# A GRU with a routed mixture of experts on one core: a slab's second weights copied by ScalarE, a third buffer for rows to be scattered, and an earlier load of x for the dense blocks

## The chip, the cores and the metric

The kernel runs on one core of a Trainium2 chip. A core has TensorE (PE in the profile; PEld is its weight loading, which runs beside the matmuls), VectorE (DVE), ScalarE (ACT), GpSimd (POOL) and SyncE (SP, which here only issues DMAs). Each has a queue of its own that runs in order. The metric is device time of one execution in microseconds; the kernel before was run seven times, and its median is 1300.95 us (1298.33 to 1306.26).

## The reference, cut to what matters

A GRU runs over x (16 sequences, 256 steps, 512 features) from the state cond. Its 4096 outputs go through a mixture of 8 experts of rank 128, two per token, and the result is added to x. All is fp32.

```python
def cell(h, x):                       # 256 times, one after the other
    i_r, i_z, i_n = jnp.split(x @ W_ih + b_ih, 3, axis=-1)
    h_r, h_z, h_n = jnp.split(h @ W_hh + b_hh, 3, axis=-1)
    r = jax.nn.sigmoid(i_r + h_r)
    z = jax.nn.sigmoid(i_z + h_z)
    n = jnp.tanh(i_n + r * h_n)
    h_new = (1.0 - z) * n + z * h
...
p = softmax(h / norm(h) @ router_w)   # over 8 experts
combine = the two largest p, divided by their sum
out = sum over e of combine[:, e] * (h @ Wa[e] @ Wb[e])
return x + out
```

## The kernel before, in words

**The GRU.** The 256 steps run one after the other in an unrolled loop (32 blocks of 8 steps). In a step (`step`, L937) PE multiplies the transposed state with the r and n weights (`into_rn`, L948), then with the z weights (`into_z`, L958); then it does that part of the next pair's x product that belongs to this step (`gate_in`, L279 and L287); then a little of the mixture's work; then it begins the next step's L948, which needs the new state. The new state comes by a chain through ACT and DVE: tanh for r (ACT L974), two DVE operations for n (L981, L982), tanh for z (ACT L979), tanh for n (ACT L983), then `zh`, `m` and `rows` (DVE L986, L988, L990) and a transpose into `hist` (DVE L993). At the end of every odd step `seed` (L259) lets ACT copy the biases into the PSUM banks of a later pair: two copies.

**The mixture.** Blocks 0 to 28 are sparse: they go in five chunks of 6, 9, 7, 4 and 3 blocks (`CHUNKS`). For each such block `Route` stores the states to DRAM, finds logits and norm (ACT Square at L638, in the fourth step of the block that follows), a softmax (ACT Exp at L308, in the fifth step, as soon as DVE has the largest logit, L305) and the top two. When a chunk is complete, `Chunk` works out a slot for each token and expert, fetches the rows back (`fetch`, L563, from SP's queue into a tile with tag `ht2`) and scatters them to slots in DRAM by indirect DMAs from POOL (`scatter`, L569). `Slab` then takes 128 slots at a time, in two units of 64 that belong to one expert each. There are 78 slabs. A slab loads its rows (L670), copies the two units' first weights out of `wa_sb` (`weights_a`, L694) and second weights out of `wb_sb` (`weights_b`, L703), each unit by a copy of 128x512 whose place depends on the expert's number; that number is read from SBUF into a register by `expert` (L684). Then it transposes (`turn`, L710), multiplies (`down`, L722), evicts (`mid`, ACT L729), multiplies again (`up`, L737), and evicts and stores (`store`, ACT L746 and SP L747). `Combine` loads x (L772), gathers each token's two results (POOL, L776), adds them (DVE L790) and stores (L794).

Blocks 29 to 31 are dense (`Moe`): all experts for all tokens (L858, transposes at L880, evicted by ACT at L887 into tiles `aT`, then L897), x loaded at L823, added at L907, stored at L908.

**What sets the order.** Every such job is an agent with a list of pieces (`plan`). At each step `choose` goes through the agents by rank (routing first, then the chunks' slabs, slabs of a chunk in their order, then the rest) and picks pieces; a piece needs its `gap` in steps and free `room` of what it `takes`, and its PE cost must fit into the step's spare 0.5 us (1.8 us where `gate_in` has nothing to do) or into a credit that makes the work finish in time. PE's part of the picked pieces is issued after the step's own matmuls (`advance(0, ...)`). The other engines' part, `then`, is issued after the step's chain (`advance(1, ...)`), in the order of the agents, and ahead of that odd step's `seed`. So an operation of a piece stands in its engine's queue between this step's chain and the next step's. `keep_order` then holds every engine to the order in which it was written. The planner works with these costs and rooms alone, not with times.

**Buffers in question.** Tag `wbg` has three buffers, `xr` three (used by `Combine` and `Moe`), and `ht2` two (the rows of `fetch`, and the `aT` tiles of `Moe`). `zero`, of 128x512, has a place of its own; it clears the slots in DRAM (`clear`, L213, in steps 6 to 45).

Of the kernel before, what the change touches and what calls it, by code (L numbers as in the profile page):

```python
# [8 lines left out]
FP = mybir.dt.float32  # L9
# [12 lines left out]
P = 128  # L22
# [23 lines left out]
def gru_moe_kernel(  # L46
# [47 lines left out]
    pe, dve, act, pool, sp = nc.tensor, nc.vector, nc.scalar, nc.gpsimd, nc.sync  # L94
    B, T, D = x.shape
    E, _, R = wa.shape
# [5 lines left out]
    HE = E // 2  # L102
# [9 lines left out]
    const = ctx.enter_context(tc.tile_pool(name="const", bufs=1))  # L112
# [12 lines left out]
    moe = ctx.enter_context(tc.tile_pool(name="moe", bufs=2))  # L125
# [29 lines left out]
    for side, src in enumerate((b_ih, b_hh)):  # L155
        for g in (0, 2, 1):
            tag = ("xg", "wbg")[side]
# [19 lines left out]
    wb_sb = const.tile([P, E, D], FP, name="wb_sb")  # L177


    zero = const.tile([P, 512], FP, name="zero")  # L180
    pool.memset(zero, 0.0)
    ones = const.tile([P, 1], FP, name="ones")
    pool.memset(ones, 1.0)
# [173 lines left out]
    class Early:  # L357
# [5 lines left out]
        def load(self):  # L363
            m = self.m
            if self.x is not None:
                return
            self.x = slb.tile([P, D], FP, tag="yg1", bufs=2, name=f"xe_{m}")
            for j in range(NJ):
                for s in range(2):
                    p0 = 32 * j + 16 * s  # L370
                    sp.dma_start(
                        self.x[p0 : p0 + B, 0:P],
                        x[:, 2 * m + s, j * P : (j + 1) * P],
                    )
# [40 lines left out]
        def plan(self):  # L415
            pieces = [
                Piece(then=[("load",)], takes="early"),
                Piece(gap=2, then=[("turn",)], takes="at"),
            ] + [
                Piece(gap=0, cost=c, pe=[("into", what, q)])  # L420
                for what, c in (("rn", 0.43), ("z", 0.22))
                for q in range(NQ)
            ] + [Piece(then=[("store",)], gives="early")]
            pieces[2].gap, pieces[2].takes = 1, ["ps"]
            pieces[9].then, pieces[9].gives = [("keep",)], ["ps", "at"]
            return pieces
# [19 lines left out]
    class Chunk:  # L446
# [112 lines left out]
            self.w = [whi, wlo]  # L559

        def fetch(self, k):
            ht = moe.tile([P, D], FP, tag="ht2", bufs=2, name=f"ht2_{self.c}_{k}")
            sp.dma_start(ht, self.rows[k].rearrange("b t d -> (b t) d"))  # L563
            self.ht = getattr(self, "ht", {})
            self.ht[k] = ht
# [93 lines left out]
    class Slab:  # L659
# [19 lines left out]
            if n == ch.n_slabs - 1:  # L679
                x_users[ch.c % 2] = ch.loads  # L680

        def expert(self, u):
            k = NU * self.n + u
            return pool.value_load(  # L684
                self.chunk.expert[0:1, k : k + 1], min_val=0, max_val=E - 1
            )

        def weights_a(self):
            self.wa = slb.tile(
                [P, NU, NQ, R], FP, tag="wag", bufs=3, name=f"wag_{self.name}"  # L690
            )
            for u in range(NU):
                e = self.expert(u)
                pool.tensor_copy(  # L694
                    self.wa[:, u, :, :],
                    wa_sb[:, :, bass.ds(e, 1), :].rearrange("p q e r -> p (q e) r"),
                )

        def weights_b(self):
            self.wb = slb.tile([P, NU, D], FP, tag="wbg", bufs=3, name=f"wbg_{self.name}")  # L700
            for u in range(NU):
                e = self.expert(u)
                pool.tensor_copy(  # L703
                    self.wb[:, u, :],
                    wb_sb[:, bass.ds(e, 1), :].rearrange("p e f -> p (e f)"),
                )
# [97 lines left out]
    class Moe:  # L804
# [14 lines left out]

        def load(self):  # L820
            i = self.i
            self.xr = moe.tile([P, D], FP, tag="xr", bufs=3, name=f"xr_{i}")
            sp.dma_start(self.xr, x[:, i * TS : (i + 1) * TS, :])  # L823

        def route(self):
# [57 lines left out]
            self.ps["t", s] = ps  # L883

        def evict(self, s):
            self.aT[s] = moe.tile([P, HE, P], FP, tag="ht2", name=f"aT_{self.i}_{s}")
            act.copy(  # L887
                self.aT[s].rearrange("p e t -> p (e t)"),
                self.ps.pop(("t", s)),
            )  # L890
# [19 lines left out]
        def plan(self):  # L910
            pieces = [
                Piece(then=[("prep",)], takes="hc a"),
                Piece(cost=0.6, pe=[("route",)], then=[("soft1",)], gives="a"),
                Piece(cost=0.86, pe=[("down", 0, 0)], then=[("soft2",)], takes="ps"),
                Piece(cost=0.86, pe=[("down", 0, 1)], then=[("soft3",)], takes="a"),
                Piece(gap=0, cost=0.86, pe=[("down", 0, 2)]),
                Piece(gap=0, cost=0.86, pe=[("down", 0, 3)], then=[("scale", 0)],
                      gives="ps"),
            ] + [Piece(gap=0, cost=0.86, pe=[("down", 1, q)]) for q in range(NQ)] + [
                Piece(cost=0.6, pe=[("trans", 0)], then=[("evict", 0)],  # L920
                      takes="ps aT", gives="ps"),
                Piece(cost=0.6, pe=[("trans", 1)], then=[("evict", 1)],
                      takes="ps", gives="ps a hc"),
            ] + [Piece(gap=0, cost=0.86, pe=[("up", e)]) for e in range(E)]
            pieces[6].takes = ["ps"]
            pieces[9].then, pieces[9].gives = [("scale", 1)], ["ps"]
            pieces[12].gap, pieces[12].takes = 1, ["ps"]
            pieces[14].then, pieces[14].takes = [("load",)], ["xr"]
            pieces[19].then, pieces[19].gives = [("store",)], "ps aT xr".split()
            return pieces  # L930


# [207 lines left out]
    for i in range(NB):  # L1140
# [26 lines left out]
        if i < n_sparse:  # L1167
            ch = chunks[-1]
            k = i - (ends[ch.c] // TS - ch.k)
# [55 lines left out]
```

## Time and profile before

The profiled execution took 1297.87 us; its span, from the first to the last instruction, is 1296.1 us. It is one execution, 3.1 us below the median of the seven.

| what | from the profile |
|---|---|
| median of 7 runs | 1300.95 us |
| profiled execution, its span | 1297.87 us, 1296.1 us |
| granted TensorE clock, mean | 0.992 |
| PE busy, PEld busy | 1245.3 us, 895.8 us |
| DVE, ACT, POOL busy | 754.2 us, 386.4 us, 379.0 us |
| of POOL: copies at L694, at L703 | 156 for 100.7 us, 156 for 99.3 us |
| first L948 on a computed state; last | 38.8 us; 1234.7 us |

A group line of the profile reads: line, engine, operation, the tile written, an arrow, the tiles read, the shape, how often; then the busy time in us and the mean of one in ns; then how long the engine had been idle just before them, and what ended that idle time. A timeline line reads: start in us, length in us, engine, line, operation, tiles, shape, how many were merged; in brackets the idle time before it and its releaser. A line of the waits reads: who waited, for whom, us in total, times, the longest. A busy PE is not PE at its limit: its matmuls overlap and their ends are modelled.

### The profile page before, as it was taken

The page shows a single profiled execution, that of the slowest core. Times are in us where ns is not written, and L with a number is a line of the kernel's source. Part 1 is how long each engine was busy: PE and PEld are TensorE (multiplying, and loading weights), DVE is VectorE, ACT ScalarE, POOL GpSimd, SP SyncE. Part 2 cuts the span into 40 slices and gives each one's busy share as a digit, 9 for nine tenths or more (in the row PEclk, how much of TensorE's full clock was granted, in tenths as well). Part 3 has the DMA queues.
Part 4 walks back from the last instruction along what each step waited for, and adds up shares of the span by engine and source line. Part 5 has one row for each costly group of instructions (what it writes and reads, how often), then busy time and mean ns, then how long its engine had stood idle before and what let it go on. Part 6 is the DMA issues. An engine that isn't in the chain of part 4 may idle for free.

```text
span 1296.1 us, 73564 instructions
## 1 busy us (share of the span) xinstructions
PE 1245.3 (96%) x32494; PEld 895.8 (69%) x32494; DVE 754.2 (58%) x2691; ACT 386.4 (30%) x1338; POOL 379.0 (29%) x668
## 2 busy tenths in 40 slices
PE   6899999999999999999999999999998988989998
PEld 3577777776777777777777777777786767766753
DVE  0455555565655555556556665566566766676643
ACT  1222222322333333233333333333333323333220
POOL 2000000023311111112424332225245554465453
PEclk7999999999999999999999999999999999999999
DMA  8532422124221112212535433225355765565454
GB/s 201 147 119 87 132 74 89 52 83 136 74 61 49 48 52 61 57 48 76 192 101 152 142 105 85 60 93 182 96 146 159 207 214 150 171 183 164 142 177 129
DMA packets 142300, 152.17 MB, mean 117 GB/s; under 512 B 21846, under 2 KB 98710, under 8 KB 141980
## 3 DMA queue, kind: packets, MB, share of 16 engines
q1 hardware_dynamic: 132560, 117.01, 31.2%
q0 software_dynamic: 9280, 30.42, 7.3%
q8 instruction: 254, 4.16, 1.4%
q14 instruction: 66, 0.54, 0.1%
q10 hardware_dynamic: 140, 0.05, 0.0%
HBM read 82.11 MB, written 65.27 MB: 114 GB/s over the span
## 4 chain that ended last, share of the span: by engine, by line
PE 87%; DVE 7%; DMA 3%; issue 1%; ACT 1%; SPq 0%; POOL 0%; POOLq 0%; ACTq 0%; DVEq 0%
PE rn L948 35%; PE z L958 17%; PE rn L279 14%; PE z L287 7%; PE at_ps L722 4%; PE y_ps L737 4%; DVE rows L990 1%; PE a_ps L858 1%; PE gi L387 1%; DVE zh L986 1%; PE o_ps L897 1%; DVE m L988 1%; DMA whh<-in_L_cond_W_hh_dram 1%; PE rt L351 1%; DVE hist L993 1%
## 5 line engine op out<-in xcount | busy, mean ns | idle before, releaser
L948 PE MATMUL rn<-whh,hist 128*32 128x256 f32 x8160 | 497.3, 383 | 29.2 <-DVE hist L993 27.8
L948 PEld LDWEIGHTS rn<-whh,hist 128*32 128x32 f32 x8160 | 251.8, 110 | 207.0 <-DVE hist L993 57.6
L279 PE MATMUL rn<-wih,xT 128*32 128x256 f32 x3712 | 291.8, 382 | 9.7 <-DMA wih<-in_L_cond_W_ih_dram 7.9
L981 DVE SCALAR_TENSOR_TENSOR n<-r,rn 128x128 f32<-128x128 f32 x256 | 73.5, 287 | 352.4 <-ACT r L974 351.4
L958 PE MATMUL z<-whh,hist 128*32 128x128 f32 x8160 | 274.1, 273 | 0.0
L958 PEld LDWEIGHTS z<-whh,hist 128*32 128x32 f32 x8160 | 238.2, 110 | 42.5 <-issue 1.4
L974 ACT ACTIVATE r<-rn 128x128 f32<-128x128 f32 x256 | 71.1, 278 | 428.4 <-PE rn L948 426.2
L287 PE MATMUL z<-wih,xT 128*32 128x128 f32 x3712 | 193.5, 274 | 0.0
L287 PEld LDWEIGHTS z<-wih,xT 128*32 128x32 f32 x3712 | 126.7, 111 | 77.5 <-issue 2.2
L703 POOL COPY wbg<-wb_sb 128x512 f32 x156 | 99.3, 647 | 107.8 <-PE y_ps L737 90.4
L279 PEld LDWEIGHTS rn<-wih,xT 128*32 128x32 f32 x3712 | 115.9, 111 | 11.6 <-DMA wih<-in_L_cond_W_ih_dram 5.0
L986 DVE SCALAR_TENSOR_TENSOR zh<-z,h 128x128 f32<-128x128 f32 x255 | 83.9, 329 | 66.9 <-ACT z L979 65.2
L694 POOL COPY wag<-wa_sb 128x512 f32 x156 | 100.7, 655 | 63.8 <-PE at_ps L722 45.9
L979 ACT ACTIVATE z<-z 128x128 f32<-128x128 f32 x256 | 71.1, 278 | 153.8 <-PE z L958 153.8
L640 POOL TENSOR_TENSOR nrm<-ss,half 128x1 f32<-128x1 f32 x29 | 16.3, 563 | 342.9 <-ACT ht L638 321.8
L722 PE MATMUL at_ps<-xgT,wag 128*32 128x64 f32 x4992 | 90.2, 219 | 4.0 <-issue 1.6
L722 PEld LDWEIGHTS at_ps<-xgT,wag 128*32 128x32 f32 x4992 | 84.1, 110 | 8.5 <-issue 3.4
L990 DVE SCALAR_TENSOR_TENSOR rows<-zh,m 128x128 f32<-128x128 f32 x256 | 82.9, 324 | 8.9
L737 PE MATMUL y_ps<-wbg,at 128*32 128x256 f32 x1248 | 87.2, 380 | 0.1
L993 DVE STREAM_TRANSPOSE hist<-rows 128x128 f32<-128x128 f32 x256 | 79.8, 312 | 8.7
L1001 DVE STREAM_TRANSPOSE h<-hist 128x128 f32<-128x128 f32 x256 | 79.7, 311 | 8.7
L988 DVE SCALAR_TENSOR_TENSOR m<-z,n 128x128 f32<-128x128 f32 x256 | 82.3, 322 | 1.0 <-ACT n L983 0.7
(136 smaller groups left out, 1042.1 us busy)
## 6 DMA issues: line engine op xcount, KB each, us to landing
xg<-x_slots SPq DMA_DIRECT2D x312, 64.0 KB
y_slots<-y SPq DMA_DIRECT2D x78, 256.0 KB
ht<-H SPq DMA_DIRECT2D x58, 256.0 KB
x_slots<-zero SPq DMA_DIRECT2D x40, 256.0 KB
x<-in_x_dram SPq DMA_DIRECT2D x256, 32.0 KB
xr<-in_x_dram SPq DMA_DIRECT2D x32, 256.0 KB
out_dram<-xr SPq DMA_DIRECT2D x32, 256.0 KB
H<-rows SPq DMA_DIRECT2D x232, 32.0 KB
```

What stands on the lines that cost most here:

```text
L279: pe.matmul(rn[32 * j : 32 * j + 32, 0 : 3 * P].rearrange("p (g d) -> p g d", g=3)[:, 0:3:2, :], lhsT=xts[m][:, q, :], rhs=w[:, 0:3:2, j, ...
L287: ins = pe.matmul(zb[32 * j : 32 * j + 32, 0:P], lhsT=xts[m][:, q, :], rhs=w[:, 1, j, :], start=False, stop=(q == NQ - 1), skip_group_chec ...
L694: pool.tensor_copy(self.wa[:, u, :, :], wa_sb[:, :, bass.ds(e, 1), :].rearrange("p q e r -> p (q e) r"),)
L703: pool.tensor_copy(self.wb[:, u, :], wb_sb[:, bass.ds(e, 1), :].rearrange("p e f -> p (e f)"),)
L722: pe.matmul(self.ps[c32, us], lhsT=self.wa[:, u, q, c32], rhs=self.xt[:, q, us], start=(q == 0), stop=(q == NQ - 1),)
L737: pe.matmul(self.ps[c32, half], lhsT=self.at[:, c32], rhs=self.wb[:, 32 * c // U, half], start=True, stop=True,)
L948: pe.matmul(rn[32 * j : 32 * j + 32, 0 : 2 * P].rearrange("p (g d) -> p g d", g=2), lhsT=hT[:, q, :], rhs=w(q, j)[:, 0:3:2, :], start=Fals ...
L958: pe.matmul(zb[32 * j : 32 * j + 32, 0:P], lhsT=hT[:, q, :], rhs=w(q, j)[:, 1, :], start=False, stop=(q == NQ - 1), skip_group_check=True,)
L986: dve.scalar_tensor_tensor(zh, z, 1.0, hrow, ALU.add, ALU.mult)
L988: dve.scalar_tensor_tensor(m, z, 1.0, n, ALU.subtract, ALU.mult)
L990: dve.scalar_tensor_tensor(hn, zh, 0.5, m, ALU.mult, ALU.subtract)
L993: dve.transpose(hist[:, t, :, lo : lo + 32], hn.rearrange("p (q c) -> p q c", q=NQ))
```

## The change

A slab's `weights_b` is issued on ACT in place of POOL: the two reads of an expert's number and the two copies. `weights_a` stays on POOL. Tag `ht2` gets three buffers; `zero` becomes the first tile in that ring, and the dense blocks' x goes through it too, so that `xr` is left to `Combine` alone. The dense blocks' load of x moves from the third `up` piece (14) to the second transpose piece (11), which is one planner step sooner, behind the second `evict`, and takes no room any more. `CHUNKS`, `ROOM` and all else stay.

```diff
-    zero = const.tile([P, 512], FP, name="zero")
+    zero = moe.tile([P, 512], FP, tag="ht2", bufs=3, name="zero")
...
         def fetch(self, k):
-            ht = moe.tile([P, D], FP, tag="ht2", bufs=2, name=f"ht2_{self.c}_{k}")
+            ht = moe.tile([P, D], FP, tag="ht2", bufs=3, name=f"ht2_{self.c}_{k}")
...
-        def expert(self, u):
+        def expert(self, eng, u):
             k = NU * self.n + u
-            return pool.value_load(
+            return eng.value_load(
...
-                e = self.expert(u)
+                e = self.expert(pool, u)
                 pool.tensor_copy(
                     self.wa[:, u, :, :],
...
-                e = self.expert(u)
-                pool.tensor_copy(
+                e = self.expert(act, u)
+                act.copy(
                     self.wb[:, u, :],
...
         def load(self):
-            self.xr = moe.tile([P, D], FP, tag="xr", bufs=3, name=f"xr_{i}")
+            self.xr = moe.tile([P, D], FP, tag="ht2", bufs=3, name=f"xr_{i}")
...
-            self.aT[s] = moe.tile([P, HE, P], FP, tag="ht2", name=f"aT_{self.i}_{s}")
+            self.aT[s] = moe.tile([P, HE, P], FP, tag="ht2", bufs=3, name=f"aT_{self.i}_{s}")
...
-            pieces[14].then, pieces[14].takes = [("load",)], ["xr"]
-            pieces[19].then, pieces[19].gives = [("store",)], "ps aT xr".split()
+            pieces[11].then.append(("load",))
+            pieces[19].then, pieces[19].gives = [("store",)], "ps aT".split()
```

## The prediction

> **What bounds the kernel now.** The page's chain ends on PE for 87% of the span, so the first question is whether PE is full or waits. The second view is the timeline, here the change from one step to the next:
>
> ```profile
> 1062.22 1.93 PE L948 MATMUL rn<-whh,hist 128*32 128x256 f32 x32 [1.93 <-DVE hist L993]
> ...
> 1063.43 0.30 ACT L308 ACTIVATE ex<-ls,mx 128x8 f32<-128x8 f32 x1 [3.65 <-DVE mx L305]
> 1063.64 0.19 ACT L308 ACTIVATION_READ_ACCUMULATOR ex<-ls,mx 128x1 f32 x1
> 1064.22 0.28 ACT L974 ACTIVATE r<-rn 128x128 f32<-128x128 f32 x1 [0.40 <-PE rn L948]
> ...
> 1066.63 1.93 PE L948 MATMUL rn<-whh,hist 128*32 128x256 f32 x32
> 1066.85 0.27 ACT L729 COPY at<-at_ps 128x128 f32<-128x128 f32 x1 [1.27 <-PE at_ps L722]
> 1067.01 0.49 ACT L259 COPY rn<-gl 128x384 f32<-128x384 f32 x1
> 1067.53 0.27 ACT L259 COPY z<-gl 128x128 f32<-128x128 f32 x1
> 1068.63 0.28 ACT L974 ACTIVATE r<-rn 128x128 f32<-128x128 f32 x1 [0.83 <-PE rn L948]
> ```
>
> ACT's r begins 2.00 us after PE's L948 (1064.22 against 1062.22), and the next L948 begins 4.41 after the last (1066.63). From r to r this 4.40 us comes back in most of the first hundred steps, with and without work for the mixture: it is the chain's own length. So in such a step a late r delays the next step by as much; PE's filler only covers a delay where a step is longer because PE was last. 256 x 4.40 is 1126 us; the loop ran from 38.8 to about 1239, so some 70 us are steps that are longer. One cause is seen in a third view, the groups by line:
>
> ```profile
> L703 POOL COPY wbg<-wb_sb 128x512 f32 x156 | 99.3, 647 | 107.8 <-PE y_ps L737 90.4
> L986 DVE SCALAR_TENSOR_TENSOR zh<-z,h 128x128 f32<-128x128 f32 x255 | 83.9, 329 | 66.9 <-ACT z L979 65.2
> L990 DVE SCALAR_TENSOR_TENSOR rows<-zh,m 128x128 f32<-128x128 f32 x256 | 82.9, 324 | 8.9
> ...
> L988 DVE SCALAR_TENSOR_TENSOR m<-z,n 128x128 f32<-128x128 f32 x256 | 82.3, 322 | 1.0 <-ACT n L983 0.7
> ```
>
> Undisturbed, the three take 291, 291 and 283 ns in the timeline. Where POOL copies beside them they take longer:
>
> ```profile
> 1075.33 0.66 DVE L986 SCALAR_TENSOR_TENSOR zh<-z,h 128x128 f32<-128x128 f32 x1 [0.26 <-ACT z L979]
> 1075.92 0.69 DVE L988 SCALAR_TENSOR_TENSOR m<-z,n 128x128 f32<-128x128 f32 x1
> 1076.64 1.13 DVE L990 SCALAR_TENSOR_TENSOR rows<-zh,m 128x128 f32<-128x128 f32 x1
> ```
>
> In that stretch POOL had L703 copies from 1074.69 to 1075.85 and L694 copies from 1075.80 on.
>
> **Gain: POOL's copies leave DVE's chain.** The means give (329-291)x255 + (322-283)x256 + (324-291)x256 = 9.7 + 10.0 + 8.4 = 28 us lost on these three, all on the chain. Laid over POOL's rows, 9.1 us of it stand beside L703 copies alone, 4.2 beside L703 and another POOL operation; the rest is L694's and others'. I take 13 us: L703's part, with the shared part whole, since what is left on POOL then runs with less backlog. Bounds: 0 (L694 copies move into the freed time and meet the same DVE operations) and 28 (all collisions come of backlog).
>
> **Cost: ACT's copies stand between the tanh of n and the next r.** All 78 slabs' pairs move. In POOL's queue a read of an expert's number is four sequencer operations, of 288, 152, 18 and 46 ns at the median, and paces the copies:
>
> ```profile
> 1232.54 1.31 POOL L694 COPY wag<-wa_sb 128x512 f32 x2
> ```
>
> The second copy starts 1.31 - 0.61 = 0.70 us after the first. ACT's own 128x512 copies run 0.53 from start to start where nothing is between:
>
> ```profile
> 1242.35 0.59 ACT L746 COPY y<-y_ps 128x512 f32<-128x512 f32 x1 [0.32 <-PE y_ps L737]
> 1242.88 0.59 ACT L887 COPY aT<-aT_ps 128x512 f32<-128x512 f32 x1
> ```
>
> So I count, from the start of the ACT instruction ahead: 0.70 to the first copy, 0.70 to the second, 0.53 until the next instruction, 1.93 in all, and 1.40 for each further slab. ACT never read a register or a register's address here, so this is a price from POOL's rows. Bounds: the reads run ahead and cost nothing (1.06 for two copies), or each read waits until the copy ahead is over (0.7 + 0.6 from copy to copy; the longest read in the trace took 1143 ns).
>
> Which steps? The planner's rules, followed step by step, put 74 pairs into 67 steps of the loop and 4 behind it; ACT's rows give what stands ahead of them.
>
> (a) Ten steps, 12 slabs: the fifth step of a block, with Exp ahead. Exp waits for DVE's L305, which comes after the state, so it ends late: in the first fence at 1063.64, then 1063.64 + 1.93 = 1065.57 against an r at 1064.22: 1.35 late. Eight such are 10.8, two with two slabs 2 x 2.75 = 5.5: 16 us.
>
> (b) Sixteen odd steps with an `at` eviction ahead, which waits for PE's filler, and the two seeds behind: in the fence 1066.85 + 1.93 = 1068.78, the seeds 0.52 + 0.27 more, r at 1069.57 in place of 1068.63: 0.94 late. Where PE has the `at` piece first, the eviction is earlier and little is lost. Row by row the sixteen are 11.1 us late, of which steps with PE last hide 0.8: 10.3 us. The seeds are 1.8 us late too; PE's `gate_in` behind them then starts some 0.5 us late, inside the delay of r.
>
> (c) Three odd steps with two slabs, or with Square ahead and no `at`: 2.4 + 2.4 + 1.8 = 6.6 us.
>
> (d) Twenty-five even steps with `at` ahead and no seeds: 0.22 + 1.93 = 2.15 against 2.00, in the steps where `at` waited; 1.2 us in all.
>
> (e) Thirteen steps with neither: the copies follow the tanh of n at 3.05 after L948, end at 4.98 (5.8 with seeds), and r is due at 6.40: 0. The cover is 0.6 us.
>
> The sum is 16 + 10.3 + 6.6 + 1.2 = 34 us. With reads for nothing the same rows give 16.5, with reads that wait 77.
>
> Two sentences of the Trainium skill bear on this. The trace has ACT busy for 30% of the span, so by its share 156 copies would fit in for nothing; "Perfetto Trace Analysis", section "Optimizing Scalar/DVE Operations", says that an unsaturated ScalarE may still cause bubbles on other engines, and advises to break its instructions up; by the share the sum would be 13 us faster, by the rows above it is slower. The trace's register read of 288 ns can be set beside "Runtime: NRT & Kernel Launch", section "Instruction fetch mechanics", which gives about 200 ns for a register read from HBM; by it, as an estimate, copies would be 0.09 us closer and the cost some 5 us less; the row is what I use.
>
> **The third buffer.** SP waits in order for scatters to let go of `ht2`, and POOL for the rows:
>
> ```profile
> SPq L563 <- DMA x_slots<-ht,ilo: 67.3, 13, 12.1
> ```
>
> With two buffers a fetch waits for the scatter issued in the same step, with three for that of the step before, so most of the 67 us goes. Behind it stand x loads, stores and slab loads; PE's waits on these are about 1 us each, and POOL's 39.7 us of waits for `ht` end no PE wait either. I take 0 (up to 3 us of fewer late POOL copies). `zero`'s clears end before step 46, the first fetch comes later: 0.
>
> **The dense loads.** Three DMAs of the same size go one planner step sooner on SP. The ring holds two `aT` and one x per block, so a load waits for the block before to be stored: that store is issued at 1259.26 and 1276.26, the loads' uses are at 1275.54 and 1291.61. What is behind such a load on SP (other stores and loads of `Combine`) waits a few us at most. Tail after the loop: ACT has about 10.6 us of work in 61; four slabs' copies shift evictions by some tenths. I take 0.5 us.
>
> **The sum.** 34 - 13 + 0 + 0.5 = 21.5 us on 1297.87: 1319.4. The median lies 3.1 above the profiled execution: 1322.5.
>
> **Rivals.**
> - Forecast, ACT's price and POOL's relief as taken: 1322.5, from about 1305 (26 - 22) to 1343 (46 - 4). Chance 0.77.
> - The reads on ACT wait for the copies ahead: 77 - 13 = 64, so 1365. For it: on POOL some reads took up to 1143 ns beside a copy. Against: the median is 288 beside running copies. Chance 0.07.
> - A wash: reads run ahead (16.5) and relief is 13 to 18: 1300 to 1304. That the third buffer frees nothing belongs here too, as I count it for nothing. Chance 0.10.
> - Faster: backlog is the cause of nearly all collisions. 28 of relief against 16.5 is -11.5: 1289. Its place is DVE L986 to L990 in the last 300 us, where POOL is busiest (147 us of 285 from 950 to 1235). It decides once the relief exceeds ACT's cost by 4 us. Against: half of POOL's copies stay, and (a) is late by the order of the queue whatever a read costs. Chance 0.06.
>
> About 0.3% (4 us) is what a measurement can tell from no change. Faster 0.06, the same 0.09, slower 0.85. The range 1302 to 1345 holds the forecast's own bounds and the upper half of the wash; it leaves out 0.07 + 0.06 + 0.05.
>
> **What would show it.** In the profile after: ACT copies of `wbg`, 0.70 apart in pairs; r's idle time no longer ended by PE in the steps of (a) and (b), with L948 to L948 some 1 to 1.4 us longer there and PE waiting for `hist`; means of L986, L988 and L990 near 310 ns; SP's wait at L563 under 15 us. It is wrong if the reads overlap the instruction ahead, if L694's copies collide as often as both did, or if the time in the tail changes by more than 2 us.

## The result, and the profile after

The kernel after takes 1311.61 us (median of 19 runs, 1307.16 to 1315.25), the kernel before 1301.34 us (46 runs on the same chips): ratio 1.0074 [1.0063, 1.0085]. It is slower, as forecast, but by 10.3 us and not by 21.5. Its profiled execution took 1310.17 us with a span of 1308.4 us, 12.3 us more than that of before; the granted clock is 0.992 in both. From line 181 on every line of the kernel after carries a number one higher.

First the chain that ended last, by engine:

```profile
PE 78%; DVE 8%; ACT 5%; DMA 3%; issue 3%; SPq 2%; ACTq 1%; POOL 0%; POOLq 0%; DVEq 0%
```

Before, PE held 87% of it and ACT 1%. Part of what PE held has gone to ACT and its queue, and the line list of the page puts 2% of the span on the new copies. The group of r before, and then the groups by line of after:

```profile
L974 ACT ACTIVATE r<-rn 128x128 f32<-128x128 f32 x256 | 71.1, 278 | 428.4 <-PE rn L948 426.2
```

```profile
L704 ACT COPY wbg<-wb_sb 128x512 f32 x156 | 96.4, 619 | 34.7 <-issue 30.6
...
L991 DVE SCALAR_TENSOR_TENSOR rows<-zh,m 128x128 f32<-128x128 f32 x256 | 78.5, 307 | 8.9
...
L987 DVE SCALAR_TENSOR_TENSOR zh<-z,h 128x128 f32<-128x128 f32 x255 | 77.4, 304 | 63.2 <-ACT z L980 62.7 <-issue 0.3
L989 DVE SCALAR_TENSOR_TENSOR m<-z,n 128x128 f32<-128x128 f32 x256 | 76.3, 298 | 5.8 <-ACT n L984 5.4
...
L975 ACT ACTIVATE r<-rn 128x128 f32<-128x128 f32 x256 | 70.8, 277 | 346.0 <-PE rn L949 345.6
```

Two things moved against each other. The DVE means fell from 329, 322 and 324 ns to 304, 298 and 307: (25 x 255 + 24 x 256 + 17 x 256) ns is 16.9 us, the gain. And ACT waited for PE before r for 346 us in place of 426: ACT arrives later at r, because copies stand ahead of it. The timeline shows both kinds of step in which this happens:

```profile
1067.60 1.93 PE L949 MATMUL rn<-whh,hist 128*32 128x256 f32 x32
...
1068.81 0.30 ACT L309 ACTIVATE ex<-ls,mx 128x8 f32<-128x8 f32 x1 [2.26 <-DVE mx L306]
1069.01 0.19 ACT L309 ACTIVATION_READ_ACCUMULATOR ex<-ls,mx 128x1 f32 x1
...
1069.46 1.28 ACT L704 COPY wbg<-wb_sb 128x512 f32 x2 [0.26 <-issue]
...
1070.65 0.27 ACT L975 ACTIVATE r<-rn 128x128 f32<-128x128 f32 x1
...
1072.22 0.27 ACT L730 COPY at<-at_ps 128x128 f32<-128x128 f32 x1 [0.31 <-PE at_ps L723]
...
1072.88 1.28 ACT L704 COPY wbg<-wb_sb 128x512 f32 x2 [0.40 <-issue]
...
1072.96 1.93 PE L949 MATMUL rn<-whh,hist 128*32 128x256 f32 x32 [0.81 <-DVE hist L994]
...
1074.07 0.48 ACT L260 COPY rn<-gl 128x384 f32<-128x384 f32 x1
...
1074.58 0.27 ACT L260 COPY z<-gl 128x128 f32<-128x128 f32 x1
...
1074.96 0.28 ACT L975 ACTIVATE r<-rn 128x128 f32<-128x128 f32 x1
```

The first step is of class (a): Exp waits for DVE, the copies wait for Exp, and r comes 3.05 us after L949 (1070.65 against 1067.60) where 2.00 is free of delay. PE pays at once: it stands 0.81 us for `hist` before the next L949. In the second the copies stand behind an `at` eviction, and seeds stand behind the copies. SP's wait at the fetch fell from 67.3 us to 15.4, as the third buffer promised:

```profile
SPq L564 <- DMA x_slots<-ht,ilo: 15.4, 7, 4.4
```

To say where the 12.3 us lie I cut each of 254 steps of the loop into three: from L949's weight load on the new state to r, from r to the end of `hist`, from there to the next L949. Undisturbed they are 2.00, 2.35 and 0.05 us, 4.40 together. The table sums what goes beyond that, from the rows of one profiled execution each (us).

| kernel | r late | chain longer | PE last | loop | behind the loop |
|---|---|---|---|---|---|
| before | 16.9 | 33.0 | 26.8 | 1194.3 | 63.0 |
| after | 42.3 | 15.8 | 30.8 | 1206.6 | 63.2 |
| change (rounded after the sum) | +25.5 | -17.2 | +4.1 | +12.3 | +0.3 |

The middle column holds more than DVE's three operations, for instance ACT's wait before the tanh of z. From the start of the tanh of n to the end of `hist`, where the three stand, the 254 steps take 357.1 us before and 340.4 after: 16.7 of the 17.2 us lie there.

### The profile page after: what moved, and what is told of

It reads as the page before. It is cut to its first block, busy times and chain, and to the rows that moved or that the text cites. A ratio compares the mean times of both kernels' runs of the same rounds, so it can differ in the third digit from the quotient of the medians.

```text
span 1308.4 us, 73461 instructions
## 1 busy us (share of the span) xinstructions
PE 1247.4 (95%) x32494; PEld 891.1 (68%) x32494; DVE 732.1 (56%) x2691; ACT 479.2 (37%) x1494; POOL 279.2 (21%) x512
## 4 chain that ended last, share of the span: by engine, by line
PE 78%; DVE 8%; ACT 5%; DMA 3%; issue 3%; SPq 2%; ACTq 1%; POOL 0%; POOLq 0%; DVEq 0%
PE rn L949 31%; PE z L959 15%; PE rn L280 12%; PE z L288 6%; PE at_ps L723 4%; PE y_ps L738 4%; ACT wbg L704 2%; PE o_ps L898 2%; PE a_ps L859 2%; DVE rows L991 1%; PE gi L388 1%; DVE m L989 1%; DVE hist L994 1%; PE rt L352 1%; DMA whh<-in_L_cond_W_hh_dram 1%
## 5 line engine op out<-in xcount | busy, mean ns | idle before, releaser
L949 PE MATMUL rn<-whh,hist 128*32 128x256 f32 x8160 | 496.3, 383 | 31.0 <-DVE hist L994 27.6
L949 PEld LDWEIGHTS rn<-whh,hist 128*32 128x32 f32 x8160 | 249.8, 110 | 211.7 <-DVE hist L994 61.0
L959 PE MATMUL z<-whh,hist 128*32 128x128 f32 x8160 | 274.0, 273 | 3.6 <-issue 3.5
L959 PEld LDWEIGHTS z<-whh,hist 128*32 128x32 f32 x8160 | 237.3, 110 | 46.9 <-issue 5.2
L987 DVE SCALAR_TENSOR_TENSOR zh<-z,h 128x128 f32<-128x128 f32 x255 | 77.4, 304 | 63.2 <-ACT z L980 62.7
L704 ACT COPY wbg<-wb_sb 128x512 f32 x156 | 96.4, 619 | 34.7 <-issue 30.6
L991 DVE SCALAR_TENSOR_TENSOR rows<-zh,m 128x128 f32<-128x128 f32 x256 | 78.5, 307 | 8.9
L984 ACT ACTIVATE n<-n 128x128 f32<-128x128 f32 x256 | 77.7, 303 | 15.8 <-DVE n L983 15.6
```

The source lines that it names most:

```text
L704: act.copy(self.wb[:, u, :], wb_sb[:, bass.ds(e, 1), :].rearrange("p e f -> p (e f)"),)
L949: pe.matmul(rn[32 * j : 32 * j + 32, 0 : 2 * P].rearrange("p (g d) -> p g d", g=2), lhsT=hT[:, q, :], rhs=w(q, j)[:, 0:3:2, :], start=Fals ...
L959: pe.matmul(zb[32 * j : 32 * j + 32, 0:P], lhsT=hT[:, q, :], rhs=w(q, j)[:, 1, :], start=False, stop=(q == NQ - 1), skip_group_check=True,)
L984: act.activation(n, n, AF.Tanh)
L991: dve.scalar_tensor_tensor(hn, zh, 0.5, m, ALU.mult, ALU.subtract)
```

## The experiments

On the chips of all experiments but first_in_loop the kernel before takes 1372 to 1376 us in place of 1301, with the same code; its granted clock there is 0.981 to 0.994 over all runs (on the chip of first_in_loop 0.991 to 0.995). So only ratios to the kernel before on the same chip are compared, and the table of steps has a part of its own for such a chip further down. A ratio of 0.01 is 13.7 us there.

| kernel | ratio to before | | kernel | ratio to before |
|---|---|---|---|---|
| act_only | 1.0060 [1.0039, 1.0082] | | act_first | 1.0054 [1.0033, 1.0076] |
| act_only_b | 1.0052 [1.0034, 1.0070] | | act_first_b | 1.0057 [1.0038, 1.0076] |
| rest_only | 1.0078 [1.0053, 1.0102] | | first_no_ring | 0.9965 [0.9949, 0.9980] |
| rest_only_b | 1.0117 [1.0100, 1.0134] | | first_no_ring_b | 0.9973 [0.9950, 0.9996] |
| after_b | 1.0146 [1.0125, 1.0166] | | first_in_loop | 0.9964 [0.9950, 0.9979] |
| before_b | 1.0003 [0.9983, 1.0023] | | ring_only | 1.0107 [1.0072, 1.0142] |
| no_copy | 0.9881 [0.9853, 0.9910] | | ring_only_b | 1.0109 [1.0074, 1.0144] |
| no_reads | 0.9923 [0.9902, 0.9944] | | dense_only | 1.0015 [0.9992, 1.0037] |
| pool_twice | 1.0186 [1.0157, 1.0215] | | ring_spaced | 1.0028 [0.9999, 1.0058] |

### The halves of the change

My theory was that ACT's copies make the whole difference and that the third buffer and the dense loads make none. The rival was that these cost something too. act_only has the copies alone:

```diff
-    e = self.expert(u)
-    pool.tensor_copy(self.wb[:, u, :], ...)
+    e = self.expert(act, u)
+    act.copy(self.wb[:, u, :], ...)
```

> Against before: ScalarE takes over the second weights, nothing else changes. Theory (the whole result is ScalarE's later r against fewer GpSimd collisions on VectorE's chain; the ring and the earlier loads give nothing): +9 to +13 us, as in the whole change, ratio 1.007 to 1.010. Rival (the third buffer gives part of the relief, since some steps without any copy became shorter and one Square came earlier): without it +14 to +18 us, ratio 1.011 to 1.014.

rest_only has all the rest, with the copies on POOL:

```diff
-    zero = const.tile([P, 512], FP, name="zero")
+    zero = moe.tile([P, 512], FP, tag="ht2", bufs=3, name="zero")
...
-            ht = moe.tile([P, D], FP, tag="ht2", bufs=2, name=f"ht2_{self.c}_{k}")
+            ht = moe.tile([P, D], FP, tag="ht2", bufs=3, name=f"ht2_{self.c}_{k}")
...
-            self.xr = moe.tile([P, D], FP, tag="xr", bufs=3, name=f"xr_{i}")
+            self.xr = moe.tile([P, D], FP, tag="ht2", bufs=3, name=f"xr_{i}")
...
-            pieces[14].then, pieces[14].takes = [("load",)], ["xr"]
+            pieces[11].then.append(("load",))
```

> Against before: the ring of three, zero in it, and the dense blocks' x sooner, with GpSimd copying as before. Theory: 0 to -1 us, ratio 0.999 to 1.000; SyncE's wait for scatters still falls from 67 to about 15 us. Rival (the third buffer gives part of the relief): -3 to -6 us, ratio 0.995 to 0.998, with fewer microseconds lost on VectorE's chain.

Both were run again, and with them the kernel after and the kernel before as kernels of their own (no edit to either).

> ScalarE's copies without the ring and the earlier loads, once more. Where the kernel before takes about 1301 us: +9 to +13 us if the ring gives nothing, +14 to +18 us if it gives part of the relief.

> The ring and the earlier loads without ScalarE's copies, once more: in the first run of it the kernel before took 1372 us on that chip, 5% above its 1301 elsewhere, and engines stood still for want of instructions around the scatters. On a chip where the kernel before takes about 1301 us: 0 to -4 us (ratio 0.997 to 1.000) if the ring gives nothing or a little; +8 to +12 us (1.006 to 1.009) if the ring itself costs what it cost in the first run.

> The whole change beside its parts on one chip. On a chip like that of the first comparison: ratio 1.0074 again. On one like that of the first four experiments: about the sum of the parts measured there, 1.006 and 1.008, so 1.012 to 1.016, if the parts add up.

> The kernel before itself, for its profile on these chips: ratio 1.00. If engines that stand still for want of instructions around the scatters make up the 70 us between 1373 and 1301, the profile has such idle time without a releaser, but less of it than the kernels with the ring of three.

The copies cost 1.0052 to 1.0060, the rest 1.0078 and 1.0117, both 1.0146. act_only lies below both ranges that were expected of it and rest_only above both of its own. On these chips the parts add up, as was expected of after_b, and the larger one is the part that I had put at nothing. That also means that 1.0146 here and 1.0074 in the result are not the same sum; the last group of experiments is about this.

### How large the relief is

no_copy leaves out the choice of the expert for the second weights: `up` multiplies by a fixed expert's block of `wb_sb` in place, and nobody copies.

```diff
-    rhs=self.wb[:, 32 * c // U, half],
+    rhs=wb_sb[:, (NU * self.n + 32 * c // U) % E, half],
```

> The kernel before without any copy of the second weights on any engine: the second product reads a fixed expert's weights in place (the choice of the expert is left out). This is the relief alone, with no cost on ScalarE. Theory (the traces: 17 us less on VectorE's chain and 6 us from earlier r): -17 to -23 us, ratio 0.983 to 0.987. Rival (the relief is what was forecast): -10 to -14 us, 0.989 to 0.992.

pool_twice is the whole change with each `wag` copy made twice:

```diff
+    for _ in range(2):
         pool.tensor_copy(self.wa[:, u, :, :], ...)
```

> The whole change, but each copy of the first weights on GpSimd is made twice (same data, same place), so GpSimd has again as many copies as before the change, while ScalarE's part is untouched. Theory (GpSimd's copies beside VectorE's chain were what the change relieved): the relief of 17 to 22 us goes and the time is +25 to +35 us against before, ratio 1.019 to 1.027. Rival (the relief has another cause, as the third buffer): the time stays within 4 us of the whole change, ratio 1.005 to 1.011.

no_copy gives 0.9881, 16 us of 1373, between its two expected ranges: POOL's second copies, with their reads and whatever waits for them, cost the kernel before that much. Its groups by line (the file is shorter, so these are zh, rows and m again under other numbers):

```profile
L980 DVE SCALAR_TENSOR_TENSOR zh<-z,h 128x128 f32<-128x128 f32 x255 | 78.6, 308 | 106.0 <-ACT z L973 97.1 <-issue 8.9
...
L984 DVE SCALAR_TENSOR_TENSOR rows<-zh,m 128x128 f32<-128x128 f32 x256 | 77.2, 302 | 8.9
L982 DVE SCALAR_TENSOR_TENSOR m<-z,n 128x128 f32<-128x128 f32 x256 | 74.1, 290 | 1.4 <-ACT n L977 0.9 <-issue 0.2
```

They stand at 329, 310 and 307 ns in before_b. In pool_twice the collisions come back in part, by the same view:

```profile
L992 DVE SCALAR_TENSOR_TENSOR rows<-zh,m 128x128 f32<-128x128 f32 x256 | 82.6, 323 | 8.9
L988 DVE SCALAR_TENSOR_TENSOR zh<-z,h 128x128 f32<-128x128 f32 x255 | 78.3, 307 | 83.9 <-ACT z L981 73.5 <-issue 9.8
L990 DVE SCALAR_TENSOR_TENSOR m<-z,n 128x128 f32<-128x128 f32 x256 | 77.8, 304 | 6.3 <-ACT n L985 5.4 <-issue 0.2
```

Against after_b (301, 305, 295) these are (22 x 256 + 2 x 255 + 9 x 256) ns, 8.4 us, for 156 added copies, and from the tanh of n to the end of `hist` the steps take 346.7 us against 338.5. So the added copies bring back part of what the moved ones took away. The ratio, 1.0186, is 0.4% above after_b's and just under the expected 1.019. It doesn't price the collisions by themselves: in these two executions PE was last for 11 us more in pool_twice, while the time from r to the tanh of z was 22 us shorter in all.

### What the reads of an expert's number cost

no_reads is act_only with a fixed expert for each unit, so it leaves out the choice of the expert as well; ACT makes the same 156 copies, but reads no register.

```diff
-    e = self.expert(act, u)
-    act.copy(self.wb[:, u, :], wb_sb[:, bass.ds(e, 1), :]...)
+    e = (NU * self.n + u) % E
+    act.copy(self.wb[:, u, :], wb_sb[:, e, :])
```

> ScalarE copies the second weights as in the change, without the ring, but of a fixed expert, so no expert's number is read on ScalarE (the choice of the expert is left out). Theory (the copies' place costs, and the reads between them about half): ScalarE's lateness falls from about 31 to about 15 us, so -3 to -9 us against before, and 12 to 16 us below the run with reads. Rival (the reads run beside the copies and cost next to nothing): +4 to +10 us, as with reads.

0.9923 against no_copy's 0.9881: copies alone cost 6 us. act_only lies 1.3% above no_reads, so the reads cost about 18 us; ACT's whole price on these chips is 24 us. The reads are the larger part of the price, though no engine counts them as busy; the expectation had them at about half. The two kernels ran on different chips of the slower kind, each beside the kernel before.

### The place in ACT's queue

The prediction put the cost on the order of the queue: copies stand behind evictions that wait for PE or DVE, though they themselves need nothing of the step. If so, the same copies ahead of these evictions should be nearly free, since ACT is idle there. act_first is the whole change with this order:

```diff
 def advance(phase, picked):
+    if phase:
+        for a, p in picked:
+            if ("weights_b",) in p.then:
+                a.weights_b()
     for a, p in picked:
         for what, *args in (p.then if phase else p.pe):
-            getattr(a, what)(*args)
+            if what != "weights_b":
+                getattr(a, what)(*args)
```

> The whole change, but a step's copies of the second weights stand first among ScalarE's work of that step, ahead of Exp, Square and the evictions, so right behind the tanh of n. Theory (a copy costs by its place in the queue): they start about 3.1 us after the step's first matmul, end at about 5.0, and the next r is due at 6.4; only the four steps with two slabs are late, by under 1 us each. The 17 us of relief on VectorE's chain stay: -10 to -17 us against before, ratio 0.987 to 0.992. Rival (ScalarE's copies cost by their number or disturb the chain wherever they stand): +5 to +12 us, ratio 1.004 to 1.009.

> ScalarE's copies first in their step, once more, for the same reason. Where the kernel before takes about 1301 us: -10 to -17 us (0.987 to 0.992) if a copy costs by its place in the queue; +5 to +12 us (1.004 to 1.009) if it costs wherever it stands.

first_no_ring has the same order with the buffers and dense loads of before:

> ScalarE's copies first in their step, with two buffers, zero and the dense loads as before. Theory (the copies cost by their place; the ring of three costs by itself on the chips of these runs, where the kernel before takes about 1373 us): -5 to -12 us there, ratio 0.991 to 0.996; where it takes 1301 us, -10 to -17 us, 0.987 to 0.992. Rival (a copy on ScalarE costs wherever it stands): +5 to +10 us.

> The same kernel as first_no_ring (ACT's copies at the head of the step's work, buffers as before), again. If its 0.9965 is more than a chance of one chip: 0.993 to 0.999. If the place in the queue is worth nothing: 1.005 as act_only.

The order takes the whole change from 1.0146 to 1.0054 and 1.0057, and the copies alone from 1.0052 and 1.0060 to 0.9965 and 0.9973: the sign turns. By itself act_first lies in the range of its rival, since its expectation had put the third buffer at nothing; it is first_no_ring, without that buffer, that decides. It gained a little less than was expected of it. Behind the loop, though, first_no_ring took 69.2 us where before_b took 64.0. In first_in_loop the order holds within the 256 steps only:

```diff
-    if phase:
+    if phase and now <= T:
...
-            if what != "weights_b":
+            if what != "weights_b" or now > T:
```

> ACT's copies at the head of a step's work within the 256 steps, in the old order behind them; buffers as before. first_no_ring's loop was 9.6 us shorter than that of the kernel before on the same chip and its tail 5.2 us longer (69.2 against 64.0). If the order in the tail is what made the tail longer: ratio 0.991 to 0.995, tail near 65 us. If the tail is longer because of what the loop leaves over for it: 0.996 to 0.998 as first_no_ring.

It fell on a chip where the kernel before takes 1300.54 us; it takes 1295.83, 0.9964. The stretch behind the loop is back at 63.5 us, so the order there seems to have made it longer; but the sum is not better than first_no_ring's, because the loop gained 6.3 us here against 9.6 there, by one execution of each. That part of the expectation missed. Its timeline and the group of r:

```profile
1071.44 0.30 ACT L983 ACTIVATE n<-n 128x128 f32<-128x128 f32 x1
...
1072.01 1.28 ACT L703 COPY wbg<-wb_sb 128x512 f32 x2 [0.27 <-issue]
...
1072.80 1.93 PE L948 MATMUL rn<-whh,hist 128*32 128x256 f32 x32
...
1073.20 0.58 ACT L746 COPY y<-y_ps 128x512 f32<-128x512 f32 x1
1073.68 0.27 ACT L729 COPY at<-at_ps 128x128 f32<-128x128 f32 x1
...
1073.84 0.49 ACT L259 COPY rn<-bias 128x384 f32<-128x384 f32 x1
...
1074.36 0.27 ACT L259 COPY z<-bias 128x128 f32<-128x128 f32 x1
...
1074.80 0.28 ACT L974 ACTIVATE r<-rn 128x128 f32<-128x128 f32 x1 [0.17 <-PE rn L948]
```

```profile
L974 ACT ACTIVATE r<-rn 128x128 f32<-128x128 f32 x256 | 70.9, 277 | 382.0 <-PE rn L948 380.7 <-issue 1.2
```

The copies start 0.57 us after the tanh of n, while DVE still makes the state. Even with two evictions and two seeds behind them, ACT still waits 0.17 us for PE before r, 2.00 us after L948. By the steps: r late 19.1 us (42.3 in after), chain 16.2 (15.8 in after), PE last 35.2. The relief is kept, ACT's price is gone, and PE takes back 8.4 us of it against before.

### The third buffer and the dense loads

These two were 0 in my sum. ring_only is rest_only without its last two edits (x stays in `xr` and is loaded in piece 14). dense_only keeps the earlier load, gives x one buffer of its own and `ht2` two:

```diff
-            self.xr = moe.tile([P, D], FP, tag="ht2", bufs=3, name=f"xr_{i}")
+            self.xr = moe.tile([P, D], FP, tag="xd", bufs=1, name=f"xr_{i}")
...
-            ht = moe.tile([P, D], FP, tag="ht2", bufs=3, name=f"ht2_{self.c}_{k}")
+            ht = moe.tile([P, D], FP, tag="ht2", bufs=2, name=f"ht2_{self.c}_{k}")
```

> Three buffers of tag ht2 with zero as the first tile of the ring, POOL copying as before, the dense blocks' x in tag xr and loaded in piece 14 as before. If the third buffer is what cost rest_only its 0.8 to 1.2% (scatters closer together, and engines standing still beside them): ratio 1.007 to 1.012 to the kernel before, POOL L570 scatters back to back, waits of over 5 us on an engine that name no instruction. If the earlier dense load is what cost: 0.998 to 1.002.

> Two buffers of tag ht2 as before, with zero as the ring's first tile; the dense blocks' x in one buffer of its own, loaded in piece 11 without taking room; POOL copying as before. If the third buffer is the cost: 0.998 to 1.002. If the earlier dense load is the cost (it stands on SP's queue until the block before is stored, with stores and loads of Combine behind it): 1.007 to 1.012, with the excess in the last 100 us.

ring_spaced is rest_only with a chunk's scatters two planner steps apart. Its slabs stay where they were, so some of them load rows that are scattered only later; the operations are the same.

```diff
     pieces[2 + m].then.append(("scatter", m))
+    if m:
+        pieces[2 + m].gap = 2
```

> rest_only with the scatters of a chunk two planner steps apart in place of one, so that the third buffer can't bring them together. If the density of scatters is the cost: 0.999 to 1.004, and waits that name no instruction as in the kernel before or shorter. If it is the earlier dense load, or a cost of the third buffer that doesn't depend on the spacing: 1.007 to 1.012 as in rest_only.

> The same kernel as ring_only. Its cost of 1.07% was measured on a chip where the kernel before takes 1372 us and where engines stand still for want of instructions beside scatters. If the cost belongs to that standing still, and the run falls on a chip where the kernel before takes about 1300 us: 0.997 to 1.003, with no step of over 9 us at the scatters. If the third buffer costs by itself: 1.007 to 1.012 on such a chip too. On a chip of 1372 us it only repeats: 1.007 to 1.014.

It is the buffer: 1.0107 and 1.0109 alone, the earlier load 1.0015 with an interval that holds 1, and with the scatters spaced 1.0028 (the weaker proof, since some slabs there no longer wait for scatters). The timeline of ring_only has the place:

```profile
284.00 1.20 POOL L570 DMA_INDIRECT x_slots<-ht,ihi  x1 [8.03 <-DVE ilo L526]
...
285.32 0.28 ACT L975 ACTIVATE r<-rn 128x128 f32<-128x128 f32 x1 [2.77 <-PE rn L949]
...
285.51 0.99 POOL L570 DMA_INDIRECT x_slots<-ht,ilo  x1 [0.31 <-issue]
...
286.81 0.98 POOL L570 DMA_INDIRECT x_slots<-ht,ihi  x1 [0.31 <-issue]
286.82 0.45 PE L288 MATMUL z<-wih,xT 128*32 128x128 f32 x4 [0.31 <-issue]
...
289.37 0.97 POOL L570 DMA_INDIRECT x_slots<-ht,ihi  x1 [0.30 <-issue]
...
291.93 0.98 POOL L570 DMA_INDIRECT x_slots<-ht,ihi  x1 [0.30 <-issue]
...
292.86 0.28 ACT L980 ACTIVATE z<-z 128x128 f32<-128x128 f32 x1 [7.26 <-remote]
```

Eight scatters run without a pause, and ACT waits 7.26 us before the tanh of z for something that the profile can't name ("remote"; PE's z matmuls, L959, had ended at 285.73), while PE takes its matmuls in groups of one to five with gaps of "issue". That step takes 12.8 us; in dense_only, where the fifth scatter waits 2.57 us for its rows, 7.6, in ring_spaced 8.7. Now the same step and the same scatters in the kernel after, in the execution of the result:

```profile
283.33 1.20 POOL L570 DMA_INDIRECT x_slots<-ht,ihi  x1 [8.03 <-DVE ilo L526]
...
284.26 0.28 ACT L975 ACTIVATE r<-rn 128x128 f32<-128x128 f32 x1 [2.37 <-PE rn L949]
...
284.84 0.99 POOL L570 DMA_INDIRECT x_slots<-ht,ilo  x1 [0.31 <-issue]
...
285.13 0.28 ACT L980 ACTIVATE z<-z 128x128 f32<-128x128 f32 x1 [0.60 <-PE z L959]
...
286.14 0.98 POOL L570 DMA_INDIRECT x_slots<-ht,ihi  x1 [0.30 <-issue]
...
287.42 0.97 POOL L570 DMA_INDIRECT x_slots<-ht,ilo  x1 [0.30 <-issue]
...
288.67 0.28 ACT L975 ACTIVATE r<-rn 128x128 f32<-128x128 f32 x1 [3.06 <-PE rn L949]
```

Scatters as close together (the first six of eight), and ACT's z follows r by 0.87 us, and r follows r after 4.41. So the buffer's price seems to hang on the chip. That is argued from one execution: ring_only_b was meant to meet a faster chip, but the kernel before takes 1375.5 us on the one it met, and no run has the buffer alone on a faster chip. All steps in which a scatter starts exceed 4.40 us by 19.6 us together in before and 14.7 in after (executions of the result), by 53.3 in before_b, 56.7 in dense_only and 65.1 in ring_only. A second part of the price is PE's clock: inside the loop the profile of ring_only has eight stretches, 30.7 us in all, in which the granted clock is 0.50, against three of 10.2 us in dense_only and two of 6.8 us in before_b. The steps of the slower chip, by the same cut as above:

| kernel | r late | chain longer | PE last | loop |
|---|---|---|---|---|
| before_b | 39.3 | 67.1 | 39.5 | 1263.5 |
| dense_only | 37.1 | 69.6 | 38.8 | 1263.1 |
| ring_only | 52.9 | 69.3 | 40.0 | 1279.8 |
| act_only_b | 75.1 | 53.1 | 31.7 | 1277.5 |
| no_copy | 45.9 | 51.4 | 36.0 | 1250.8 |
| no_reads | 48.5 | 54.3 | 35.7 | 1256.2 |
| first_no_ring | 45.1 | 51.4 | 39.8 | 1253.9 |

With one execution a row it shows the three effects roughly apart: the chain is 13 to 16 us shorter wherever POOL's second copies are gone, 10 to 12 of them between the tanh of n and the end of `hist`; ACT's price is in the first column and goes with the reads or with the place; the buffer's is in the first column too (52.9 against 37.1 of dense_only). One execution may lie some us off its median (act_only_b's loop is 14 us longer here, its median 7), so the sizes are taken from the ratios.

## Why the prediction was right in direction and wrong in size

| term of the sum | forecast | measured in the result's two executions |
|---|---|---|
| (a) behind Exp | +16 | r later by 12.8 |
| (b) behind `at`, seeds behind | +10.3 | 11.3 |
| (c) two slabs, or Square | +6.6 | 3.7 |
| (d) even steps with `at` | +1.2 | 3.1, of which 2.4 in one step |
| (e) neither | 0 | 0.3 |
| relief of DVE's chain | -13 | chain shorter by 17.2 |
| r sooner in steps without a copy ahead | not in the sum | -5.8 |
| PE last | -0.8 (inside (b)) | +4.1 |
| third buffer, dense loads | 0 | no rise at the scatters (14.7 against 19.6) |
| behind the loop | +0.5 | +0.3 |

**ACT's price was nearly right in place and size.** 34 was forecast, 31.2 us of later r were measured, in the classes in which they were expected. Class (a) came out lower by a slip that the timeline of after shows: I counted 1.93 us from the start of the accumulator's read (1069.01), but the register read begins with the dispatch of Exp itself, and r follows Exp's start by 1.84 (1070.65 - 1068.81), 0.3 us sooner than forecast. Such a step is 1.05 us late and not 1.35. In (c) one of the three steps was not late at all, since Square came earlier there. In (d) the sum had overlooked that one even step with `at` ahead has two slabs: its r is 2.4 us late. The pacing of 0.70 us taken from POOL's rows was 0.66 on ACT (1.28 - 0.62). That the reads cost about 17.5 us of it (34 - 16.5) is borne out: 18 us by no_reads, though on the other chips.

**The step that failed is the gain.** Its mechanism was right and its size was not. I took 13 us by counting only collisions beside L703 copies, and named 28 as the upper end. The chain became 17.2 us shorter in the result's executions, 16.7 of it from the tanh of n on. The remaining POOL copies collide less often, too: with half of the copies gone, 16.9 of the 28 us went. I had seen this possibility ("less backlog") and gave it nothing beyond the shared 4.2 us. On the slower chips the same stretch became only 10 to 12 us shorter.

**Two terms were not in the sum at all.** In the steps without a copy ahead of r, r comes 5.8 us sooner in total, and PE is last for 4.1 us more; the prediction put both at nothing without a reason. Three steps of before make 5.4 of the 5.8, as its timeline shows:

```profile
991.14 3.32 PE L948 MATMUL rn<-whh,hist 128*32 128x256 f32 x32 [2.17 <-DVE hist L993]
...
1056.22 0.63 ACT L638 ACTIVATE ht<-ht 128x512 f32<-128x512 f32 x1 [3.57 <-DMA ht<-H]
...
1161.69 3.21 PE L948 MATMUL rn<-whh,hist 128*32 128x256 f32 x32 [2.02 <-DVE hist L993]
```

In two of them L948 takes 3.32 and 3.21 us in place of 1.93: from 991.52 and from 1162.19 on, the granted clock is 0.50 for 3.41 us. In the third, Square waits 3.57 us for its rows, and two evictions and two seeds stand behind it. After has two such stretches of half clock as well, in other steps (from 947.17 and 1100.77 on), which cost 2.4 us there; the rest of the 5.8 comes in smaller pieces. So this term is largely what the two executions happened to hold, and not shown to be an effect of the change. Why PE is last for longer stays open. All together 31.2 - 17.2 - 5.8 + 4.1 is 12.3, against 21 in the sum for the loop: 4.2 of the 8.7 between them is the gain, 2.8 ACT's price, and the two omitted terms make 1.7.

**The third buffer at 0 was right for the result, as far as its profile shows, and right by luck.** I had argued from PE's and POOL's waits in one execution, where POOL's waits for `ht` end no wait of PE. That other engines could stand still beside denser scatters was nowhere in the prediction; on a chip like those of the experiments the whole change would have cost 1.46% and the reason would have been another.

**The rivals.** Reads that wait for the copies ahead (1365) are excluded: the second copy starts 0.66 us after the first, while that one takes 0.62. The faster rival needed a relief of 28; it was 17. The wash needed reads that run ahead; no_reads shows what that would have given, 0.9923 on its chips. The result lies between the wash and the forecast. ACT is busy for 37% of the span after the change, and yet the kernel is slower with 156 copies on it, and ACT's share of the chain rises from 1% to 5%. What the sentence of the Trainium skill that the prediction weighed ("Perfetto Trace Analysis", section "Optimizing Scalar/DVE Operations") starts from, a ScalarE that is not saturated and still causes bubbles, is borne out by that; its advice, to break instructions up, no run here tries.

## What to carry to other kernels

Work that is moved to an idle engine is priced by its place in that engine's queue, not by the engine's share: moving the same copies costs 0.55% behind evictions that wait and gains 0.3% ahead of them. Count what an operation needs before it can start (here two register reads, three quarters of the price on the slower chips) and not only its busy time. And where a change makes transfers denser, try it on more than one chip before the term is put at nothing.

## What was not expected of the hardware

- **Chips differ, and differ most beside scatters.** The same kernel takes 1301 us on some chips and 1372 to 1376 on others, with nearly the same time behind the loop (63.0 and 64.0 us), and with 0.992 and 0.994 as the granted clock of the two profiled executions. On the slower ones engines wait for releasers that the profile can't name, 43.5 us of it before ACT's z in before_b, where the profile of before on the first chips has no such wait; steps with a scatter are 34 us longer there (53.3 against 19.6), and a third buffer costs 1.1%. That it is instructions that come late is only argued, from PE's gaps that end by "issue"; no run here shows what holds them up.
- **A stretch of half clock follows some of PE's pauses.** In before the granted clock is 0.50 for 3.41 us twice in the loop, 0.4 and 0.5 us after PE ended pauses of 2.17 and 2.02 us, and L948 then takes up to 3.32 us in place of 1.93. What sets it off was not measured.
- **A register read on ACT begins when the instruction ahead is dispatched**, as far as the starts show, and not when it ends: from the `at` eviction's start at 1072.22 to the first copy are 0.66 us, to the second 0.66 more, though the eviction takes 0.27 us and the copy 0.62.
- **Beside POOL copies a DVE operation with two inputs can take two to four times as long**: 156 of them cost 16.9 us by the DVE means, and 156 other ones, added in pool_twice, 8.4 us. The Trainium skill, "SBUF — State Buffer", section "SBUF: two separate sides", describes a port pair that DVE and GpSimd hold in turn for whole instructions, among others when a DVE operation reads two SBUF operands. The 0.66 and 0.69 us of `zh` and `m` beside POOL's copies agree with that: 0.29 and a part of one copy of 0.65. The 1.13 us of `rows` is more than 0.29 and one whole copy, and no run here shows why.
